# Two transformer-like layers: layer 0's output products in two pieces around the second head's turning, layer 1's first products in another order, layer 1's outputs through ScalarE

## The chip, the core and the metric

The kernel runs on one core of one Trainium2 chip. The metric is the device time of one launch in microseconds (us); the time before is the median of three runs. One more execution was recorded by the hardware profiler, and all times of single instructions come from it.

## What is computed

All values are float32, 4 sequences of 512 tokens (2048 in all) with 512 features. Two layers each add an attention and a mixture of experts to x:

```
xn = layernorm(x)
x  = x + attention0(xn) + experts0(xn)      # layer 0
xn = layernorm(x)
x  = x + attention1(xn) + experts1(xn)      # layer 1
```

- attention0 has 16 heads of 128. Queries, local keys and values are projections of xn with RMS norm and rotation. Each head adds two contexts: a softmax over the 8 best of the compressed entries (each entry stands for 4 tokens), and a softmax over the window of the last 128 tokens. The mean of both goes through the output matrix Wo: `out = merged @ Wo + bo`.
- experts0 takes the two best of 8 experts for each token, each one matrix, weighted by a softmax.
- attention1 is plain softmax attention with 16 heads of 32: `out = ctx @ wo_w.T + wo_b`.
- experts1 is again two of 8 experts with silu, a projection of the mix, the addition of x, and an RMS norm.

## The kernel before, in words

Tokens lie in 16 row tiles of 128. TensorE multiplies and also transposes by a product with the identity; results come out in PSUM, which has 8 banks of 128 x 512 float32. VectorE (V, DVE in the profile), ScalarE (A, ACT) and GpSimd (G, POOL) empty them. Every engine works through its own list of instructions in order. A scheduler makes these lists from the program's order and moves instructions among each other within an engine, apart from those pinned by `keep_in_program_order`. Additional work (norms, logits, experts, mixing) is put in by `run0((i, place))` in layer 0 and `run1((g, kc))` in layer 1, which run the jobs written down for that place.

**Layer 0** is the loop at L1020 over 32 steps: 8 groups of 2 heads (HG = 2), and for each the 4 sequences. Three kinds of PSUM tile are used: "mm" (3 banks), "sc" (3), "tr" (2) (L73). A step makes scores and contexts of its two heads and, between them, the projections of the next step by seven smaller products (`product`, L661, in "mm"; first to fifth). Its end is what the change touches, in this order:
- `turn_context(i, 0)`: four transposes of the first head's context (L820, trc, in "tr"), and one ScalarE copy into cT (L821).
- `fourth()` and `fifth()` of the next step, with the turnings of its queries and keys (L681, L687). In steps 5 to 23 `fifth()` stands behind these turnings, elsewhere in front. `fifth()` makes the products p3 in two halves (c = 0, 1), each added into lv by VectorE (L725), which frees its bank; then four squares with a sum on ScalarE (sq_k, L564), and the rotation on VectorE (L573 to L576). In steps 0 and 1, compressed keys and values of a sequence (kv, L609) are made nearby too.
- `turn_context(i, 1)` for the second head, `run0((i, 3.5))`.
- `output(i, t)` for the four row tiles t: two accumulating products, head 0 and head 1 (L828; each is two matmul instructions in the profile), into one "mm" bank, and VectorE's add into acc (L831).

A bank of a kind is taken again when the tile three before it (for "mm") has been emptied.

**The passage to layer 1** (L1429 on): PSUM is divided anew: "mm" 3 banks, "cx" 1, and 2 double ones, "st". `values(b, t)` is the value projection of a row tile (L1146, added out by L1148). `next_layer(n)` gives a pair of functions: the norm's rows on VectorE (L221 to L236), with wo_b added by GpSimd and the tile stored, and the turning of the normalised tile (trx, L242, copied out by ScalarE, L243). `second_logits(b)` issues the router's products (L252) and their copy (L254), and returns the function that turns them (trg, L259) and adds them up on VectorE (L867, L868). L1115 and L1116 are VectorE sums of weight matrices that must have landed first (wkT among them). 

**Layer 1's main loop** is over 16 groups of 4 heads and 4 blocks of keys: scores (st, L1224), the exponential on ScalarE (pT, L1226), context (cx, L1238), the sums of the weights on VectorE (L1244), queries and keys of a coming group (qp, L1200, emptied by L1204 to L1208). At the fourth block of groups 5 to 15, `output1(b, t)` makes one row tile of the attention's output: four products (o, L1307), then `add_part` (L1296), in which VectorE adds the PSUM tile to x, fetched by DMA before (`bring`, L1292). One more call follows the loop; that makes 12. The last four tiles are made otherwise (L1477, L1488). Jobs put in between mix the experts' rows: two gathers by DMA, L1340 and L1341 on VectorE, the turning (trc, L1349, copied out by L1353), the projection (po, L1360), the add L1361 that empties it, the square on ScalarE (L1364), two steps on GpSimd (L1365, L1366), L1371 on VectorE, and `add_part` again. All of o, po, qp, trc and sm share the three "mm" banks.

Of the kernel before, what the change touches and what calls it, by code (L numbers as in the profile page):

```python
# [12 lines left out]
F32 = mybir.dt.float32  # L13
I32 = mybir.dt.int32
AF = mybir.ActivationFunctionType
ALU = mybir.AluOpType
# [4 lines left out]
P = 128  # L21
B, S, HID = 4, 512, 512
T = B * S
NT = T // P
TC = S // P
# [11 lines left out]
HG = 2  # L37
# [12 lines left out]
def two_layers(ctx: ExitStack, tc: tile.TileContext, a: dict, out: bass.AP, large: bass.AP):  # L50
# [4 lines left out]
    V, G, A, PE = nc.vector, nc.gpsimd, nc.scalar, nc.tensor  # L55
# [17 lines left out]
    def psum(tag, name):  # L73
        return ps.tile([P, 512], F32, tag=tag, name=name, bufs={"mm": 3, "sc": 3, "tr": 2}[tag])
# [32 lines left out]
    def load_out(g):  # L107
        wo = wpool.tile([P, HG, HID], F32, tag="Wo", name=f"Wo_{g}", bufs=1)
        nc.sync.dma_start(out=wo, in_=a["Wo"][ds(g * HG * D, HG * D), :].rearrange("(h p) c -> p h c", p=P))
        return wo  # L110
# [12 lines left out]
    sums_w, out_w = {}, {}  # L123
# [3 lines left out]
    acc = keep.tile([P, NT, HID], F32, tag="acc", name="acc")  # L127
# [87 lines left out]
    def layernorm(n, pool, bank, scaled=False):  # L215

        pin = tc.keep_in_program_order if n < TC else (lambda x: x)
        st = small.tile([P, 6], F32, tag="st", name=f"st_{n}")  # L220
        pin(V.bn_stats(st, acc[:, n, :]))  # L221
        mv = small.tile([P, 2], F32, tag="mv", name=f"mv_{n}")
        V.bn_aggr(mv, st)
        V.tensor_scalar(mv[:, 1:2], mv[:, 1:2], 1e-5, None, ALU.add)
        G.tensor_tensor(mv[:, 1:2], mv[:, 1:2], nhalf[:, 0:1], ALU.pow)
        if scaled:
            G.tensor_scalar(mv[:, 0:1], mv[:, 0:1], mv[:, 1:2], -1.0, ALU.mult, ALU.mult)
        made = {}

        def rows():  # L230
            tag = "ctx" if n in (2, 3) else "xn"
            xn = made["xn"] = (wk0 if n in (2, 3) else pool).tile([P, HID], F32, tag=tag, name=f"xn_{n}")
            if scaled:
                A.activation(xn, acc[:, n, :], AF.Identity, scale=mv[:, 1:2], bias=mv[:, 0:1])
            else:
                pin(V.tensor_scalar(xn, acc[:, n, :], mv[:, 0:1], mv[:, 1:2], ALU.subtract, ALU.mult))  # L236
            (nc.scalar if TC <= n < 2 * TC else nc.sync).dma_start(out=xnd[ts(n, P), :], in_=xn)

        def turn():
            xn, tr = made["xn"], bank("tr", f"trx_{n}")  # L240
            for k in range(KC):
                pin(PE.transpose(tr[:, ts(k, P)], xn[:, ts(k, P)], ident))  # L242
            A.copy(xnT[:, :, ts(n, P)], tr.rearrange("p (k t) -> p k t", k=KC))  # L243
        return rows, turn


    def logits(b, w, m, pool, name, get, bank):


        lp = bank("sc", f"lg_{name}_{b}")  # L250
        for k in range(KC):
            PE.matmul(lp[ts(k, FEW), :], lhsT=w[:, k, :], rhs=xnT[:, k, ts(b, S)], start=True, stop=True)  # L252
        lr = pool.tile([P, S], F32, tag="lr", name=f"lr_{name}_{b}", bufs=1)
        A.copy(lr, lp)  # L254

        def turn():
            tr = bank("tr", f"trg_{name}_{b}")
            for t in range(TC):
                PE.transpose(tr[:, ts(t, P)], lr[:, ts(t, P)], ident)  # L259
            get(tr.rearrange("p (t k m) -> p t m k", k=KC, m=FEW)[:, :, 0:m, :])  # L260
        return lr, turn
# [555 lines left out]
    def turn_context(i, h, ctx_, cT):  # L817
        tr = psum("tr", f"trc_{i}_{h}")
        for t in range(TC):
            PE.transpose(tr[:, ts(t, P)], ctx_[:, t, :], ident)  # L820
        A.copy(cT[:, h, :], tr)  # L821

    def output(i, t, cT):
        g, b = steps[i]
        wo = out_w[g]
        op = psum("mm", f"op_{g}_{b}_{t}")
        for h in range(HG):
            PE.matmul(op, lhsT=cT[:, h, ts(t, P)], rhs=wo[:, h, :],  # L828
                      start=(h == 0), stop=(h == HG - 1))
        n = b * TC + t  # L830
        V.tensor_tensor(acc[:, n, :], acc[:, n, :], op, ALU.add)  # L831

    def combine(ex, n):
        rs = ex.gather(n)
# [29 lines left out]
    def second_logits(b, pool, bank):  # L864
        def get(rows_):
            own = lg1[:, ts(b, TC), :]
            V.tensor_reduce(own, rows_, AX.X, ALU.add)  # L867
            V.tensor_tensor(own, own, rout["rb"].unsqueeze(1).to_broadcast([P, TC, E]), ALU.add)  # L868
        return logits(b, rout["rw"], E, pool, "r1", get, bank)[1]
# [8 lines left out]
    for b in range(1, B):  # L878
        i = b - 2
# [58 lines left out]
    def next_layer(n, pool, bank):  # L938
        make_rows, turn_ = layernorm(n, pool, bank)

        def rows():
            make_rows()

            G.tensor_tensor(acc[:, n, :], acc[:, n, :], rout["wo_b"], ALU.add)
            nc.sync.dma_start(out=accd[ts(n, P), :], in_=acc[:, n, :])
        return rows, turn_
# [10 lines left out]
    for n in range(3 * TC):  # L957
        i, t = 29 + n // TC, n % TC
# [61 lines left out]
    for i, (g, b) in enumerate(steps):  # L1020
        if b == 0:
            if g:
                out_w[g] = load_out(g)
            if g + 1 < NH // HG:
                groups[g + 1] = load_later(g + 1)
        more = i + 1 < len(steps)
        turn_last = turn_keys
        now = qkT
        cT = qp.tile([P, HG, S], F32, tag="cT", name=f"cT_{g}_{b}", bufs=1)
        nc.sync.dma_start(out=cv0s[i % 2][96:P, 0:D], in_=cv[0:32, b, 0:D])  # L1030
        em0, lT0 = scores(i, 0, now)
        turn_last(1)
        if more:
            load_sums(i + 1)
            qkT, sums_x, first, second, third, fourth, fifth, turn_queries, turn_keys = project(i + 1)
            first()
            sums_x()
            if b == 2 and g + 1 in groups:
                groups[g + 1][0][0] = load_block(g + 1, "wA")
        run0((i, 0))  # L1040
        em1, lT1 = scores(i, 1, now)
        sT0 = turn(i, 0, em0)
        run0((i, 1))
        if more:
            second(0)
            turn_queries(0)
        ctx0 = context(i, 0, lT0, sT0, lv)
        if more:
            second(1)
        sT1 = turn(i, 1, em1)  # L1050
        if more:
            third()
        if b == 2 and g + 1 in groups:
            combine_weights(g + 1)
        run0((i, 2))
        ctx1 = context(i, 1, lT1, sT1, lv)
        turn_context(i, 0, ctx0, cT)
        run0((i, 3))
        if more:
            fourth()  # L1060

            for f in (lambda: turn_queries(1), lambda: turn_keys(0), fifth) if 5 <= i < 24 else (fifth, lambda: turn_queries(1), lambda: turn_keys(0)):
                f()
        turn_context(i, 1, ctx1, cT)
        run0((i, 3.5))
        for t in range(TC):
            output(i, t, cT)
        run0((i, 4))
    scratch.close()
    layer0.close()  # L1070
# [6 lines left out]
    ap_ = ctx.enter_context(tc.tile_pool(name="att1", bufs=2))  # L1077
    scratch = ctx.enter_context(ExitStack())
    rp = scratch.enter_context(tc.tile_pool(name="route1", bufs=1, side="right"))
# [18 lines left out]
    bank1 = lambda tag, name: psum1("mm", name)[:, 0, :]  # L1098
# [42 lines left out]
    def values(b, t):  # L1141
        if t == 0:
            v[b] = ap_.tile([P, TC, HID], F32, tag="v", name=f"v1_{b}")
        vp = bank1("mm", f"vp_{b}_{t}")
        for k in range(KC):
            PE.matmul(vp, lhsT=xnT[:, k, ds(b * S + t * P, P)], rhs=wa["wvT"][:, k, :],  # L1146
                      start=(k == 0), stop=(k == KC - 1))
        V.tensor_tensor(v[b][:, t, :], vp, rows["wv_b"], ALU.add)  # L1148
# [145 lines left out]
    def add_part(n, part_, way):  # L1294
        x = lies.pop((n, way))
        V.tensor_tensor(x, x, part_, ALU.add)  # L1296
        left[n] -= 1
        if left[n] == 0:
            nc.sync.dma_start(out=out_v[n], in_=x)
        elif (n, 1 - way) not in lies:  # L1300
            nc.sync.dma_start(out=accd[ts(n, P), :], in_=x)

    def output1(b, t):
        n = b * TC + t
        op = bank1("mm", f"o1_{n}")
        for jj in range(NJ):
            PE.matmul(op, lhsT=cT1[b][:, jj, ts(t, P)], rhs=wa["woT"][:, jj, :],  # L1307
                      start=(jj == 0), stop=(jj == NJ - 1))
        add_part(n, op, 0)

    r1 = Routing("r1", lg1, rp, const, bank1)
    held = {}
# [103 lines left out]
        jobs1.append((place, lambda t=t: values(1, t)))  # L1416
    run1 = schedule(jobs1)

    values(0, 0)
    norm = [next_layer(3 * TC + t, rp, bank1) for t in range(2)]  # L1420
    norm[0][0]()
    values(0, 1)
    turn_ = second_logits(B - 2, rp, bank1)
    norm[0][1]()
    norm[1][0]()
    norm.append(next_layer(3 * TC + 2, rp, bank1))
    values(0, 2)
    turn_()
    norm[1][1]()  # L1429
    norm[2][0]()  # L1430
    norm.append(next_layer(3 * TC + 3, rp, bank1))
# [7 lines left out]
    for g in range(NG):  # L1439
        b, j = groups1[g]  # L1440
# [743 lines left out]
```

## Time and profile before

| | us |
|---|---|
| three runs | 2075.61, 2073.08, 2073.09 |
| median | 2073.09 |
| the profiled execution | 2074.66 |
| its span, first to last instruction | 2072.6 |
| TensorE busy in it | 2017.7 (97%) |
| VectorE, ScalarE, GpSimd busy | 1452.0, 867.9, 754.3 |
| mean granted TensorE clock | 0.995 |

Lines of the profile begin with the line of the kernel (L828), then engine, operation and out<-in. In a timeline the first number is the start, the second the duration of the row (several instructions where it ends in x16), and the bracket tells how long the engine was idle before it and which instruction ended that. In the list of waits the three numbers are the total in us, how often, and the longest. A row of a window gives its bounds and length, then the busy us and number of instructions of PE, PEld (weight loads), DVE, ACT and POOL, the granted clock, the DMA share and GB/s.

### The profile page before, as it was taken

The page shows a single profiled execution, that of the slowest core. Times are in us where ns is not written, and L with a number is a line of the kernel's source. Part 1 is how long each engine was busy: PE and PEld are TensorE (multiplying, and loading weights), DVE is VectorE, ACT ScalarE, POOL GpSimd, SP SyncE. Part 2 cuts the span into 40 slices and gives each one's busy share as a digit, 9 for nine tenths or more (in the row PEclk, how much of TensorE's full clock was granted, in tenths as well). Part 3 has the DMA queues.
Part 4 walks back from the last instruction along what each step waited for, and adds up shares of the span by engine and source line. Part 5 has one row for each costly group of instructions (what it writes and reads, how often), then busy time and mean ns, then how long its engine had stood idle before and what let it go on. Part 6 is the DMA issues. An engine that isn't in the chain of part 4 may idle for free.

```text
span 2072.6 us, 27984 instructions
## 1 busy us (share of the span) xinstructions
PE 2017.7 (97%) x9130; PEld 1205.3 (58%) x9130; DVE 1452.0 (70%) x3543; ACT 867.9 (42%) x2600; POOL 754.3 (36%) x761
## 2 busy tenths in 40 slices
PE   6999999999999999999999999999999999999997
PEld 4666666666666666666666666666334445445442
DVE  7888967666766666676667778787596555557775
ACT  4554444444444443444444455454243432333332
POOL 4422244443423333344333444353114332332550
PEclk9999999999999999999999999999999999999999
DMA  7102133333333343234443222121317765773551
GB/s 250 68 31 62 42 118 120 143 108 103 130 130 104 109 155 103 92 135 166 183 170 116 70 76 85 42 72 62 119 51 244 263 243 196 257 243 123 158 163 52
DMA packets 98906, 267.23 MB, mean 129 GB/s; under 512 B 14400, under 2 KB 27840, under 8 KB 87488
## 3 DMA queue, kind: packets, MB, share of 16 engines
q0 software_dynamic: 27072, 148.91, 21.4%
q1 hardware_dynamic: 70528, 114.34, 16.4%
q10 hardware_dynamic: 1152, 2.10, 0.3%
q8 instruction: 75, 1.23, 0.2%
q14 instruction: 79, 0.65, 0.1%
HBM read 222.05 MB, written 42.73 MB: 128 GB/s over the span
## 4 chain that ended last, share of the span: by engine, by line
PE 81%; DVE 8%; ACT 3%; POOL 2%; DMA 2%; issue 1%; SPq 0%; ACTq 0%; POOLq 0%; DVEq 0%
PE p L661 23%; PE hp_r L518 12%; PE op L828 10%; PE st L753 4%; PE st L1224 3%; PE qp L1200 3%; PE sp L744 3%; PE cx L1238 2%; PE ca L797 2%; PE o L1307 2%; PE trm_r L506 2%; PE vp L1160 1%; PE trq L681 1%; PE trk L687 1%; PE cc L800 1%
## 5 line engine op out<-in xcount | busy, mean ns | idle before, releaser
L828 PE MATMUL op<-Wo,cT 128*128 128x512 f32 x512 | 230.6, 598 | 5.3 <-DVE lv L725 2.9
L518 PE MATMUL hp_r<-we_r,xT_r 128*128 128x512 f32 (+1 forms) x592 | 224.8, 596 | 0.0
L470 POOL DMA_INDIRECT xr_r<-xnd,rows_r x72 | 89.4, 1242 | 331.6 <-PE trm_r L506 298.2
L761 POOL TENSOR_TENSOR lT<-lT,lmask 128x512 f32<-128x512 f32 (+1 forms) x128 | 157.6, 1244 | 140.8 <-ACT lT L757 140.6
L661 PE MATMUL p<-wT,x 128*128 128x384 f32 x512 | 179.6, 493 | 0.5 <-DVE wT L119 0.5
L661 PE MATMUL p<-wB,x 128*128 128x384 f32 x512 | 175.9, 488 | 4.0 <-DVE u L717 4.0
L661 PE MATMUL p<-wA,xnT 128*128 128x384 f32 x512 | 174.0, 492 | 0.2 <-DVE u L696 0.2
L828 PEld LDWEIGHTS op<-Wo,cT 128*128 128x128 f32 x512 | 92.0, 190 | 115.0 <-issue 77.2
L564 ACT ACTIVATE sq<-qb 128x128 f32<-128x128 f32 x384 | 118.9, 310 | 93.0 <-DVE qb L710 44.9
L1226 ACT ACTIVATE pT<-st 128x1024 f32<-128x1024 f32 x128 | 123.7, 1014 | 62.7 <-PE st L1224 57.0
L518 PEld LDWEIGHTS hp_r<-we_r,xT_r 128*128 128x128 f32 (+1 forms) x592 | 83.8, 170 | 97.3 <-issue 91.8
L831 DVE TENSOR_TENSOR acc<-acc,op 128x512 f32<-128x512 f32 x128 | 87.4, 685 | 69.4 <-PE op L828 69.0
L661 PEld LDWEIGHTS p<-wB,x 128*128 128x128 f32 x512 | 93.9, 190 | 68.5 <-issue 10.2
L661 PEld LDWEIGHTS p<-wT,x 128*128 128x128 f32 x512 | 94.5, 193 | 63.5 <-issue 6.7
L661 PEld LDWEIGHTS p<-wA,xnT 128*128 128x128 f32 x512 | 95.6, 193 | 61.0 <-issue 2.9
L675 ACT ACTIVATE qb<-qb,ss 128x128 f32<-128x128 f32 x256 | 81.9, 390 | 110.7 <-POOL ss L566 108.6
L508 ACT COPY xT_r<-trm_r 128x512 f32<-128x512 f32 x72 | 41.8, 581 | 198.0 <-PE hp_r L518 188.3
L757 ACT ACTIVATE lT<-st,ss 128x256 f32<-128x256 f32 (+1 forms) x128 | 47.2, 449 | 175.4 <-PE st L753 175.3
L753 PE MATMUL st<-qkT 128*128 128x256 f32 (+1 forms) x512 | 110.4, 357 | 0.0
L534 POOL DMA_INDIRECT row_r<-yd,slot_r x64 | 74.2, 1160 | 94.0 <-DVE row_r L1341 35.8
L753 PEld LDWEIGHTS st<-qkT 128*128 128x128 f32 x512 | 93.1, 193 | 11.4 <-issue 1.4
L566 POOL TENSOR_TENSOR ss<-ss,nhalf 128x6 f32<-128x6 f32 x64 | 95.7, 1496 | 5.3
(360 smaller groups left out, 4334.2 us busy)
## 6 DMA issues: line engine op xcount, KB each, us to landing
x<-xsd SPq DMA_DIRECT2D x112, 256.0 KB, 3.1
yd<-yr_r SPq DMA_DIRECT2D x72, 256.0 KB, 3.4
wA<-in_wA SPq DMA_DIRECT2D x16, 384.0 KB, 3.6
wB<-in_wB SPq DMA_DIRECT2D x16, 384.0 KB, 7.6
xnd<-xn SPq DMA_DIRECT2D x24, 256.0 KB, 2.0
accd<-acc SPq DMA_DIRECT2D x18, 256.0 KB, 2.0
acc<-in_x SPq DMA_DIRECT2D x16, 256.0 KB, 4.9
Wo<-in_Wo SPq DMA_DIRECT2D x8, 512.0 KB, 3.6
```

The lines of the kernel that those rows point to most:

```text
L470: G.indirect_dma_start(out=out, out_offset=None, in_=src, in_offset=at_rows(idx))
L518: PE.matmul(hp[ts(h, m), :], lhsT=xT[:, k, ts(h, m)], rhs=w[:, ts(k, HID)], start=(k == 0), stop=(k == KC - 1))
L534: G.indirect_dma_start(out=x, out_offset=None, in_=self.yd, in_offset=at_rows(self.r.slot[:, k, n : n + 1]))
L564: A.activation(sq, x[:, h, :], AF.Square, accum_out=ss[:, h : h + 1])
L566: G.tensor_tensor(ss, ss, nhalf[:, 0:n], ALU.pow)
L661: PE.matmul(p, lhsT=x[:, k, ts(c, P)], rhs=w[:, k, :], start=(k == 0), stop=(k == 1))
L675: A.activation(x[:, j, :], x[:, j, :], AF.Copy, scale=sq[t][:, j : j + 1])
L753: PE.matmul(st[:, ds((t % 2) * 256, n)], lhsT=qkT[:, HG + h, ts(t, P)], rhs=qkT[:, h, ds(t * P, n)], start=True, stop=True)
L761: G.tensor_tensor(dst, dst, lmask.rearrange("p a w j -> p (a w j)")[:, 0:n], ALU.mult)
L828: PE.matmul(op, lhsT=cT[:, h, ts(t, P)], rhs=wo[:, h, :], start=(h == 0), stop=(h == HG - 1))
L831: V.tensor_tensor(acc[:, n, :], acc[:, n, :], op, ALU.add)
L1226: A.activation(pt[:, ts(pair, 2), :], st, AF.Exp, scale=SCALE1)
```

## The change

Three parts. In layer 0, `output` makes one head's product at a time and keeps the tile open between: the first-head products of row tiles 0 and 1 stand ahead of the second head's turning, that of tile 2 behind it, that of tile 3 between the second-head products of tiles 2 and 3. Three "mm" banks are open at once in that stretch. At the passage to layer 1, the first two norms are built ahead of the first value product, the logits of the third sequence are issued ahead of the second value product, and turned right behind it. In layer 1, ScalarE copies each of the 12 output tiles to SBUF, into a buffer of its own (one for all), and VectorE adds from there.

```
-    def output(i, t, cT):
+    open_ = {}
+
+    def output(i, t, h, cT):
+
         g, b = steps[i]
-        wo = out_w[g]
-        op = psum("mm", f"op_{g}_{b}_{t}")
-        for h in range(HG):
-            PE.matmul(op, lhsT=cT[:, h, ts(t, P)], rhs=wo[:, h, :],
-                      start=(h == 0), stop=(h == HG - 1))
-        n = b * TC + t
-        V.tensor_tensor(acc[:, n, :], acc[:, n, :], op, ALU.add)
+        if h == 0:
+            open_[t] = psum("mm", f"op_{g}_{b}_{t}")
+        PE.matmul(open_[t], lhsT=cT[:, h, ts(t, P)], rhs=out_w[g][:, h, :], start=(h == 0), stop=(h == HG - 1))
+        if h == HG - 1:
+            n = b * TC + t
+            V.tensor_tensor(acc[:, n, :], acc[:, n, :], open_.pop(t), ALU.add)
...
+
+        output(i, 0, 0, cT)
+        output(i, 1, 0, cT)
         turn_context(i, 1, ctx1, cT)
+        output(i, 2, 0, cT)
         run0((i, 3.5))
         for t in range(TC):
-            output(i, t, cT)
+            if t == 3:
+                output(i, t, 0, cT)
+            output(i, t, 1, cT)
         run0((i, 4))
...
-        add_part(n, op, 0)
+        o = ap_.tile([P, HID], F32, tag="o", name=f"o1s_{n}", bufs=1)
+        A.copy(o, op)
+        add_part(n, o, 0)
...
+    norm = [next_layer(3 * TC + t, rp, bank1) for t in range(2)]
     values(0, 0)
-    norm = [next_layer(3 * TC + t, rp, bank1) for t in range(2)]
     norm[0][0]()
+    turn_ = second_logits(B - 2, rp, bank1)
     values(0, 1)
-    turn_ = second_logits(B - 2, rp, bank1)
+    turn_()
     norm[0][1]()
     norm[1][0]()
     norm.append(next_layer(3 * TC + 2, rp, bank1))
     values(0, 2)
-    turn_()
     norm[1][1]()
```

## The prediction

> **What bounds the kernel.** I read the page first (busy shares, groups), then TensorE's waits, then timelines of single places. The first two lines of this fence are from the page, the rest from TensorE's waits (us in total, times, longest).
>
> ```profile
> PE 2017.7 (97%) x9130; PEld 1205.3 (58%) x9130; DVE 1452.0 (70%) x3543; ACT 867.9 (42%) x2600; POOL 754.3 (36%) x761
> ...
> L828 PE MATMUL op<-Wo,cT 128*128 128x512 f32 x512 | 230.6, 598 | 5.3 <-DVE lv L725 2.9 <-ACT cT L821 2.3
> ...
> PE op L828 <- DVE lv L725: 2.9, 4, 0.7
> PE op L828 <- ACT cT L821: 2.3, 5, 1.1
> PE po L1360 <- DVE acc L1296: 2.1, 1, 2.1
> PE qp L1200 <- DVE xnT L1296: 2.0, 1, 2.0
> PE vp L1146 <- ACT xnT L243: 1.4, 2, 0.7
> PE trc L820 <- ACT cT L821: 1.3, 1, 1.3
> ```
>
> TensorE is 97% busy, with 2072.6 - 2017.7 = 54.9 us idle, and the change adds or drops no TensorE instruction. In the two compiled orders SyncE's DMA issues stand as they stood, and GpSimd moves only a few normalisation steps. So the time moves only by the idle that it opens or closes, and by the granted clock. All waits that it could aim at are in that list: 5.3 in front of the outputs, 1.3 in front of the turnings, 4.1 behind layer 1's adds, and some 1.4 + 0.8 at layer 1's start: about 13 us, 0.6%. A matmul of 512 columns follows the one before by 0.43 us (16 of L828 take 6.9), one of 128 by 0.11. I use these paces.
>
> **Layer 0, steps 5 to 22 (18 steps): 0.** The timelines of step 10 (start, us, engine, what), first TensorE, then VectorE, then ScalarE:
>
> ```profile
> 544.69 0.81 PE L661 MATMUL p<-wB,x 128*128 128x384 f32 x2
> 545.34 0.60 PE L820 MATMUL trc<-ident,ctx 128*128 128x128 f32 x4
> 545.77 7.11 PE L828 MATMUL op<-Wo,cT 128*128 128x512 f32 x16
> ...
> 545.54 0.56 DVE L725 TENSOR_TENSOR lv<-p,u 128x384 f32<-128x384 f32 x1 [0.36 <-PE p L661]
> ...
> 545.97 0.59 ACT L821 COPY cT<-trc 128x512 f32<-128x512 f32 x1 [0.29 <-PE trc L820]
> 546.45 0.31 ACT L564 ACTIVATE sq_k<-lv 128x128 f32<-128x128 f32 x1
> ```
>
> Now, the second head's copy (L821, ends 546.56) is covered by tile 0's first-head product (0.86 from 545.77, to 546.63): hardly any stall. After, two products (1.72) run from 545.34 to 547.06, the turning to 547.50, tile 2's product to 548.36. The copy starts when ScalarE is through the four squares, which now stand ahead of it: one of them is held until 546.10 by L725, then three at 0.44 each end near 547.5. It starts at 547.8 (0.3 behind the turning), ends at 548.4: the same stall within 0.1. The three open tiles take all three "mm" banks. Tile 1 needs the bank of p3's first half (L725 ended at 545.18, wanted at 546.20), tile 2 the second's (546.10, wanted at 547.50): both in time. The last add falls where it fell. Bounds: ±0.1 a step, 18 steps, **±1.8**; I take 0, as every wanted time above has slack but the copy's.
>
> **Steps 0 and 1: +2.5.** Here the compressed keys and values (kv, L609) lay around the turning; the change puts outputs ahead of them. TensorE, then VectorE, in step 0:
>
> ```profile
> 91.72 0.60 PE L687 MATMUL trk<-ident,qb 128*128 128x128 f32 x4
> 92.16 0.39 PE L609 MATMUL kv<-wk,entT 128*128 128x128 f32 x2
> 92.56 0.66 PE L820 MATMUL trc<-ident,ctx 128*128 128x128 f32 x4
> 93.05 0.83 PE L609 MATMUL kv<-wk,entT 128*128 128x128 f32 x6
> 93.72 1.06 PE L609 MATMUL kv<-wv,entT 128*128 128x128 f32 x8
> 94.62 7.24 PE L828 MATMUL op<-Wo,cT 128*128 128x512 f32 x16
> ...
> 94.01 1.01 DVE L725 TENSOR_TENSOR lv<-p,u 128x384 f32<-128x384 f32 x2
> ```
>
> VectorE reaches L725 only at 94.01, behind L718, L719 and L652. After, tile 0 starts at 92.16 and ends its first product at 93.02, tile 1 waits for L725's first half, about 94.57: 1.5 of idle, queued in front of the turning and of kv, which used to fill it. From there 14 output matmuls (6.0) and 4 + 16 of the short ones (2.2) end near 102.8 instead of 101.7: **+1.1**. In step 1 (turning of keys ended at 138.59, L725 at 140.74) the same working ends at 149.3 instead of 147.9: **+1.4**; two transposes ahead of tile 1 fill 0.2 of it. Bounds: 0, if the stall is taken from a later wait, to +1.6 each. I take the near-full price, as VectorE waits on TensorE at the end of both steps (1.03 in front of the last add of each) and so has nothing to give back.
>
> **Other steps: +0.8.** Step 2: +0.16. Step 4: -0.36 (its turning waits 0.7 on L682 now; a product covers that). Step 23: -0.29. In 24, 25, 27 and 28 to 31 the product between was there already, and the longer way through tile 2 puts the second-head copy behind more squares or norms: +0.12 x 3, +0.48, +0.35, +0.08, +0.05. Sum **+0.8**, bounds -0.7 (only the gains) to +1.5 (only the losses). Layer 0: **+3.3**.
>
> **Layer 1's start: +0.3.** Both norms are built and the logits issued before the second values product. The turning at 1462.94 waits 0.83 for the copy of the logits (L254) and the values at 1464.27 wait 0.68 for L243; the values product (3.6) that moves ahead covers the first. But the logits' second turning (L259) then stands early, and its bank is emptied on VectorE by L867, now queued behind L1115. L1115 runs at 1461.54 and 1462.80 because wkT lands at 1461.5. So the norm's turning gets its bank near 1464.4 and the next values start at 1465.7. Against that, the wait of 0.80 at 1469.21 for xn goes. The third values product starts where it did within 0.1; with the last outputs of step 31 later, **+0.3**; bounds -1.6 (both covered waits gone) to +2.0 (all waits replaced by VectorE's queue).
>
> **Layer 1's outputs through ScalarE: -1.2.** Twelve copies of 128x512 at 0.58 (the row of L821 and L1353) are 7 us on an engine 42% busy, beside TensorE; the next ScalarE operation behind outputs 0 to 6 comes 4.1 later, so nothing queues behind the copy there. For these the add, too, already comes 0.2 after the matmuls: 0. If the cover went (ScalarE late by a whole copy), it would be 12 x 0.58 = 7 at most. Output 8 is where it can pay:
>
> ```profile
> 1972.40 0.68 DVE L1296 TENSOR_TENSOR xnT<-xnT,o 128x512 f32<-128x512 f32 x1
> 1973.00 0.67 DVE L1361 TENSOR_TENSOR xa<-xa,po 128x512 f32<-128x512 f32 x1
> 1973.13 3.12 PE L1200 MATMUL qp<-xnT,wqT 128*128 128x256 f32 x8 [2.01 <-DVE xnT L1296]
> ...
> 1974.00:1977.50 3.50, 3.50 (x10) 2.77 (x9) 0.74 (x1) 3.07 (x6) 2.42 (x4) 0.54 0.86 260
> ```
>
> The tile was ready at 1964.5, but VectorE stood in L1361, L1371 and L1244 until 1972.40, and qp waited 2.01 for the bank. The last line is one window: the granted clock is 0.54 behind that wait, which costs about 1.7 us more. After, the copy is due behind the two Exps that end at 1967.47, long before qp wants the bank (1971.1). But the next two qp tiles need the bank of the projection emptied by L1361, which stays behind the add, at 1973.7, and the gather's row sums end at 1980. I count 1.2 of the 3.7 as kept. Output 9 is alike: po waits 2.13 at 2016.60; after, it starts at 2014.4, but the following projection needs L1361 at 2023.41 to 2024.09 as now (it starts at 2024.23 today): all is lost again. Bounds: -5.8 (2.0 + 1.7 + 2.1 all kept) to +2 (nothing kept, and one low-clock stretch of 1.7 in the now longer idle at 2024). I take **-1.2**, nearer to the row of L1361.
>
> On the clock, the trace first: a wait of 2.01 was followed by 3.4 us at about half clock, one of 2.13 was not. [...]
>
> **Sum.** +3.3 + 0.3 - 1.2 = **+2.4** against the profiled execution, 2074.66 (span 2072.6 and 2.06 around it): 2077.1. That one lies 1.57 over the median of the three runs, so the median moves from 2073.09 to **2075.5**. 0.2%, about what a measurement can tell from no change, is 4.1 us: 2068.9 to 2077.2.
>
> **Rivals.**
> - Covers replace each other, as summed: 2075.5, chance 0.50, own range 2071.5 to 2077.2. This holds also the case that hardly anything moves (2073).
> - **Banks and squares decide (slower)**, 0.33. With three tiles open, any lateness of L725 or of the four squares stops TensorE in each of 18 steps, with the turning queued behind it. For it: copy and demand meet within 0.1 in my working. Against: L725 has 1.0 to spare. At 0.2 a step it is 3.6 more, 2079.1; it decides from 0.1 a step (1.8, with the 2.4: 2077.3). A low-clock stretch behind the 1.5 us stalls of steps 0 and 1, 1.7 each, comes to the same.
> - **Layer 1 keeps its gain (faster)**, 0.17: -5.8, with steps 0 and 1 absorbed later and the -0.7 of the other steps: 2073.1 - 6.5 = 2066.6. For it: each freed bank is one that TensorE waited for by name. Against: L1361 and the gathers stand where they stood.
>
> The range 2069.5 to 2080.5 takes in the first case and the nearer half of both others.
>
> **What would show it.** Right: L828 waits for L725 about 1.5 in each of steps 0 and 1, and kv runs behind it; in steps 5 to 22 the stall ahead of the second head stays under 0.1; the 2.0 at qp and 2.1 at po go, and new waits on L1361 follow within 10 us. Wrong: a wait on L821 near 0.3 in each step (slower), or a layer 1 shorter by over 3 us (faster).

## The result and the profile after

The changed kernel takes 2077.95 us (median of 16 runs, 2075.9 to 2080.85) against 2073.66 for the kernel before (16 runs, 2071.7 to 2076.01): a ratio of 1.0020, 95% interval 1.0012 to 1.0027. It is slower by 4.3 us, just over the 0.2% that was set as the bound. The forecast was 2.4 us.

First the costliest group of the page of the changed kernel, then its TensorE waits (total, times, longest) that answer to those shown of before:

```profile
L830 PE MATMUL op<-Wo,cT 128*128 128x512 f32 x512 | 236.0, 599 | 10.0 <-DVE lv L725 7.9
```

```profile
PE op L830 <- DVE lv L725: 7.9, 8, 1.5
PE po L1370 <- DVE xa L1371: 2.5, 3, 1.5
PE op L830 <- ACT cT L821: 2.1, 3, 1.3
PE trc L1359 <- DVE qk L1213: 1.4, 1, 1.4
...
PE vp L1154 <- ACT xnT L243: 1.3, 2, 0.7
...
PE trc L1359 <- DVE qk L1221: 1.1, 2, 0.9
```

The change aimed at three kinds of wait. The waits of qp and po behind layer 1's adds (2.0 and 2.1) are gone, and waits on L1371, L1213 and L1221 have come: 5.0 us at po and trc, and 0.7 more at qp, where before only L1361 had 1.6 at po:

```profile
PE po L1360 <- DVE xa L1361: 1.6, 3, 0.6
```

The wait of the turning on L821 (1.3) is gone from that name and now stands at an output product. And the outputs wait 7.9 for L725, where it was 2.9.

To see where it went, I cut TensorE's time at five points that every kernel has. The first stretch runs from the first matmul to the end of step 1's outputs, the passage from step 31's last output to the first scores of layer 1 (L1224 of before), the loop from there to the last matmul. A run of matmuls is taken to end 0.43 after its last start (16 of L828 take 6.9 in the kernel before), and the last matmul counts by its start. All numbers are us, from the profiled execution of each kernel; those below "changed" are the experiments.

| kernel | to end of step 1 | steps 2 to 27 | 28 to 31 | passage | loop | ratio of times (95%) |
|---|---|---|---|---|---|---|
| before | 142.03 | 1154.93 | 148.41 | 31.44 | 582.32 | |
| changed | 146.39 | 1154.10 | 150.13 | 32.33 | 581.14 | 1.0020 (1.0012 to 1.0027) |
| layer 0 part only | 145.22 | 1154.18 | 150.41 | 32.68 | 581.35 | 1.0016 (1.0007 to 1.0025) |
| passage only | 141.60 | 1154.95 | 148.64 | 30.24 | 580.40 | 0.9996 (0.9986 to 1.0005) |
| copies only | 141.85 | 1154.92 | 149.49 | 31.45 | 581.85 | 0.9999 (0.9990 to 1.0007) |
| changed, steps 0 and 1 as before | 142.23 | 1154.40 | 150.13 | 33.09 | 582.55 | 1.0002 (0.9993 to 1.0011) |
| changed, other banks in steps 0 and 1 | 141.63 | 1154.12 | 150.14 | 33.02 | 581.42 | 1.0005 (0.9996 to 1.0014) |
| copies only, adds on GpSimd | 141.40 | 1154.92 | 152.90 | 31.45 | 585.13 | 1.0024 (1.0014 to 1.0034) |
| pieces in 4 to 23, and passage | 141.77 | 1154.15 | 149.39 | 30.26 | 581.07 | 0.9991 (0.9982 to 1.0000) |
| the same, turning ahead of p3 | 143.66 | 1153.62 | 148.15 | 30.25 | 580.67 | 0.9982 (0.9973 to 0.9991) |

A column can be read against itself: kernels whose code agrees in a stretch show how far it varies by chance. Steps 2 to 27 repeat within 0.03 in the kernels that have the old code there, the passage within 0.02 where no low clock falls into it. With the code of before, the first stretch varies by some 0.8 in all but the last row, steps 28 to 31 by 1.1 (by 4.5 with the run with adds on GpSimd), and the loop without copies by 1.9. In the last row's first stretch, whose code is that of before, TensorE waits 1.6 for L596 at 71 us, where the kernel before has no wait.

Now the places. In the changed kernel's timeline of step 0, first TensorE, then VectorE:

```profile
93.64 1.02 PE L830 MATMUL op<-Wo,cT 128*128 128x512 f32 x2
96.11 1.12 PE L830 MATMUL op<-Wo,cT 128*128 128x512 f32 x2 [1.44 <-DVE lv L725]
97.07 0.60 PE L820 MATMUL trc<-ident,ctx 128*128 128x128 f32 x4
97.51 1.02 PE L830 MATMUL op<-Wo,cT 128*128 128x512 f32 x2
98.37 1.05 PE L609 MATMUL kv<-wk,entT 128*128 128x128 f32 x8
...
95.50 1.01 DVE L725 TENSOR_TENSOR lv<-p,u 128x384 f32<-128x384 f32 x2
```

Tile 0's product runs, tile 1's waits 1.44 for the bank that L725 empties, and the turning and all of kv are queued behind it. Set instruction against instruction, TensorE's lag behind the kernel before grows by 1.23 in step 0 and 1.53 in step 1. (It had already lost 1.5 before step 0, in the head of the kernel, where nothing was changed.) From step 5 to step 22 the lag stays at 3.81 throughout.

The steady step 10 of the changed kernel, TensorE and then the one copy on ScalarE:

```profile
549.14 1.88 PE L830 MATMUL op<-Wo,cT 128*128 128x512 f32 x4
550.86 0.60 PE L820 MATMUL trc<-ident,ctx 128*128 128x128 f32 x4
551.29 5.40 PE L830 MATMUL op<-Wo,cT 128*128 128x512 f32 x12
...
551.50 0.58 ACT L821 COPY cT<-trc 128x512 f32<-128x512 f32 x1 [0.23 <-PE trc L820]
```

Tile 2's first-head product (551.29 to 552.15) covers the copy (551.50 to 552.08), and the second head's run follows. From the first output or turning of the stretch to the scores it was 7.38 before (545.34 to 552.72); it is 7.39 now (549.14 to 556.53).

The passage, first two rows of the kernel before, then the changed kernel's TensorE, its VectorE ahead of the first wait, and the window behind the two waits:

```profile
1452.66 0.66 PE L242 MATMUL trx<-ident,xn 128*128 128x128 f32 x4 [0.80 <-DVE xn L236]
1469.21 0.66 PE L242 MATMUL trx<-ident,xn 128*128 128x128 f32 x4 [0.80 <-DVE xn L236]
...
1458.22 0.66 PE L242 MATMUL trx<-ident,xn 128*128 128x128 f32 x4 [1.19 <-DVE xn L236]
1459.55 5.40 PE L1154 MATMUL vp<-wvT,xnT 128*128 128x512 f32 x8 [0.67 <-ACT xnT L243]
...
1470.46 0.66 PE L242 MATMUL trx<-ident,xn 128*128 128x128 f32 x4 [0.45 <-DVE lg L869]
...
1456.43 0.69 DVE L221 BATCH_NORM_STATS2 st<-acc 128x6 f32<-128x512 f32 x1
1457.03 0.67 DVE L833 TENSOR_TENSOR acc<-acc,op 128x512 f32<-128x512 f32 x1
1457.62 0.54 DVE L236 TENSOR_SCALAR xn<-acc,mv 128x512 f32<-128x512 f32 x1
...
1460.00:1463.50 3.50, 3.50 (x6) 1.36 (x5) 0.00 (x0) 0.00 (x0) 0.52 (x2) 0.53 1.03 355
```

The first wait was 0.80 before (at 1452.66). The eight matmuls behind it take 5.4 instead of 3.6, and the granted clock is 0.53 there: nothing of the kind stood in the passage of before, where it is 1.00 from 1447 to 1463.

### The profile page after: what moved, and what is told of

Its sections match the earlier page's. It is cut to its first block, busy times and chain, and to the rows that moved or that the text cites. A ratio compares the mean times of both kernels' runs of the same rounds, so it can differ in the third digit from the quotient of the medians.

```text
span 2077.3 us, 27995 instructions
## 1 busy us (share of the span) xinstructions
PE 2019.2 (97%) x9130; PEld 1203.3 (58%) x9130; DVE 1452.5 (70%) x3543; ACT 876.3 (42%) x2612; POOL 755.5 (36%) x761
## 3 DMA queue, kind: packets, MB, share of 16 engines
q8 instruction: 75, 1.23, 0.2%
## 4 chain that ended last, share of the span: by engine, by line
PE 77%; DVE 8%; ACT 3%; POOL 2%; DMA 2%; issue 1%; SPq 0%; DVEq 0%; ACTq 0%; POOLq 0%
PE p L661 21%; PE hp_r L518 12%; PE op L830 10%; PE st L753 4%; PE st L1232 3%; PE qp L1208 3%; PE sp L744 2%; PE cx L1246 2%; PE ca L797 2%; PE o L1315 2%; PE trm_r L506 2%; PE vp L1168 1%; PE vp L1154 1%; PE trq L681 1%; DVE pS L1252 1%
## 5 line engine op out<-in xcount | busy, mean ns | idle before, releaser
L830 PE MATMUL op<-Wo,cT 128*128 128x512 f32 x512 | 236.0, 599 | 10.0 <-DVE lv L725 7.9
```

Source lines behind the costliest of these rows:

```text
L830: PE.matmul(open_[t], lhsT=cT[:, h, ts(t, P)], rhs=out_w[g][:, h, :], start=(h == 0), stop=(h == HG - 1))
```

## Layer 0's part alone, and the passage alone

**Layer 0's part** is the first two hunks of the change, on the kernel before.

> Only layer 0's part of the change. In the changed kernel's trace TensorE falls behind the kernel before by 1.2 us in step 0 and 1.5 in step 1, gains 0.4 each in steps 4 and 23, loses nothing in steps 5 to 22, and loses about 1.7 in steps 28 to 31. Theory (products ahead of the compressed keys' matmuls wait for a bank that VectorE frees late): all of that comes here, +3.2 to +3.6 us. Rival 1 (a new stall in each of 18 steps): the loss grows evenly over steps 5 to 22, over +4. Rival 2 (the loss is the chip's start, which has nothing to do with the change): about 0 beside the start.

Ratio 1.0016 (1.0007 to 1.0025). The lag grows by 1.27 in step 0 and 1.54 in step 1, shrinks by 0.44 over steps 2 to 4 (0.32 of it in step 4) and by 0.38 in step 23, stays flat in steps 5 to 22, and grows by 2.0 in steps 28 to 31. That is the theory's list, and no stall in each step. One thing was not on it: the passage, whose code is that of before here, takes 32.68 instead of 31.44, with the wait of 1.19 for L236 (0.80 before) and a low clock behind it (0.55 in the 3.4 us from 1458.60).

**The passage** is the last hunk alone.

> Only the passage to layer 1. Theory (the covered wait for the logits' copy returns as a wait for VectorE's L867): between +0.3 and +0.9, too little to see in the median, to be read from the trace as TensorE's lag behind the kernel before at the first queries of layer 1. Rival (this part is a gain that the late norms of layer 0's last step spoiled in the full change): -0.8 or better at that place.

The passage takes 30.24 instead of 31.44: **the rival was right**, this part gains 1.2 by itself. Its TensorE rows:

```profile
1452.44 0.65 PE L242 MATMUL trx<-ident,xn 128*128 128x128 f32 x4 [0.80 <-DVE xn L236]
1453.77 3.70 PE L1146 MATMUL vp<-wvT,xnT 128*128 128x512 f32 x8 [0.68 <-ACT xnT L243]
...
1462.98 0.66 PE L242 MATMUL trx<-ident,xn 128*128 128x128 f32 x4 [0.45 <-DVE lg L867]
```

The wait for L867 that I had expected is there, but at 0.45, since the scheduler puts L867 behind only the first of the two L1115 in this kernel; and the wait for xn at the next turning (0.80 before, at 1469.21) is gone. In the three kernels that hold all three parts, L867 (then L869) stands behind both, as I had read it from the changed kernel's order. In the two later kernels with this part and without the copies it stands behind the first only, so the copies go with the other order; no run has this part and the copies alone. The two experiments below that hold all three parts show what that costs: VectorE's rows in the first of them (the sums have line 1130 there),

```profile
1462.97 1.23 DVE L1130 TENSOR_TENSOR acc<-wkT 128x1024 f32<-128x1024 f32 x1 [0.98 <-DMA wkT<-in_wkT]
1464.23 1.23 DVE L1130 TENSOR_TENSOR acc<-acc,wqT 128x1024 f32<-128x1024 f32 x1
1465.37 0.28 DVE L869 TENSOR_REDUCE lg<-trg_r 128x32 f32<-128x128 f32 x1
```

and a wait of 1.23 for L869 at the turning, against 0.45 here. The changed kernel's own 0.45 only says that TensorE came late to the turning, in the low clock. So the parts don't add up: the gain of 1.2 belongs to this part alone, with another order on VectorE.

## The copies alone

Only the hunk in `output1`.

> Only the 12 copies through ScalarE. Theory (the wait of 2.0 at qp and of 2.1 at po go, and most comes back as waits on L1361 and on the row sums of the gathers): -1.0, between -0.5 and -1.5, at the end, with a lead of about 2.5 for some 8 us behind output 8. Rival 1 (all freed): -3.7 to -5.8. Rival 2 (the copies delay the exponentials): +0.5 or more.

Ratio 0.9999 (0.9990 to 1.0007); the loop takes 581.85. The waits of 2.0 and 2.1 are gone here too, and TensorE's waits in the loop's last part (1900 to 2060 us) are these:

```profile
PE po L1362 <- DVE xa L1363: 2.4, 2, 2.0
PE trc L1351 <- DVE qk L1205: 2.2, 1, 2.2
PE sm L1252 <- DVE pS L1244: 0.7, 1, 0.7
PE qp L1200 <- DVE xa L1363: 0.7, 1, 0.7
```

The lead behind output 8 is there too (2.4 us in the stretch from 1970), and given back 10 us later. Over all kernels but the next one, the loop takes 582.32, 581.35, 580.40, 581.07 and 580.67 without copies (mean 581.2) and 581.14, 581.85, 582.55 and 581.42 with them (mean 581.7). So the copies change the names of the waits and no gain is left; -1.0 is not borne out. The spread of 1.9 among kernels without copies is larger than what was to be measured. Part of it is the clock: the five loops without copies had six stretches of 3.4 us at half clock, the four with copies two. With 1.7 us taken off for each (an estimate: half of 3.4), the loops take 577.3 to 580.6 without copies and 580.2 to 581.4 with them. So the copies seem to cost about what they save in low clock; no run separates the two.

To learn what holds these places, the adds behind the copies went to GpSimd. (It adds from the copy in SBUF. Other than the description of the kernel before has it, none of the 761 GpSimd instructions in its trace reads a PSUM tile: VectorE and ScalarE alone empty them.)

```
-    def add_part(n, part_, way):
+    def add_part(n, part_, way, V=V):
...
-        add_part(n, op, 0)
+        o = ap_.tile([P, HID], F32, tag="o", name=f"o1s_{n}", bufs=1)
+        A.copy(o, op)
+        add_part(n, o, 0, G)
```

> The 12 copies alone, and the adds behind them on GpSimd in place of VectorE. In all runs with copies so far the waits of 2.0 (qp) and 2.1 (po) went, and waits for L1361, L1205 and L1213 on VectorE of the same sum came. Theory A (VectorE's queue is the limit at outputs 8 and 9): without 0.68 of add ahead of L1361 the new waits shrink by 0.5 to 0.7 each, main loop 580 to 581. Theory B (the gathers and the chain of the norm set these places): the same waits within 0.3, or longer ones, as GpSimd's add (about 1.28) delays the gathers that it issues; main loop 582 or more.

Ratio 1.0024, loop 585.13: theory B. The waits of this kernel in the same part of the loop:

```profile
PE po L1362 <- DVE xa L1363: 3.5, 3, 2.5
PE trc L1351 <- DVE qk L1205: 2.7, 1, 2.7
PE trc L1351 <- DVE qk L1213: 2.3, 2, 1.2
```

Taking 0.68 of add from VectorE at each output did not shorten them. GpSimd's add at output 8 runs from 1979.32 to 1980.59, and the next gather that GpSimd issues begins only at 1980.75. So 0.68 less on VectorE is not enough to shorten these waits when 1.27 more stands in front of the gathers on GpSimd. The run changes both at once, so it doesn't show that VectorE's load has no part, and whether the gathers and GpSimd's chain also set these places in the kernel before was not tried. (Steps 28 to 31, whose code is that of before, also took 3.9 longer in this run than in the other four kernels with that code on average, with a low clock, 0.50 to 0.52 from 1438.20 to 1445.00, behind a wait of 1.89 for L770 in step 31.)

## Steps 0 and 1

The whole change, with the order of before for the first two steps:

```
+        if i >= 2:
             output(i, 0, 0, cT)
             output(i, 1, 0, cT)
             turn_context(i, 1, ctx1, cT)
...
+        else:
+            turn_context(i, 1, ctx1, cT)
+            run0((i, 3.5))
+            for t in range(TC):
+                output(i, t, 0, cT)
+                output(i, t, 1, cT)
+            run0((i, 4))
```

> The whole change, but steps 0 and 1 keep the order of before. Theory: 2.7 us less than the whole change, so about +0.6 against before beside the noise of the start; no wait of L830 on L725 in steps 0 and 1. Rival (the late time in steps 0 and 1 would have been lost at a later wait anyway): within 1 us of the whole change.

2074.54, ratio 1.0002 (0.9993 to 1.0011), against 1.0020 for the whole change; the first stretch is 142.23. The time lost in these two steps is not lost anyway: without it the kernel ends sooner.

Is it the bank, or the later place of kv? The same order, with other banks:

```
-            open_[t] = psum("mm", f"op_{g}_{b}_{t}")
+            open_[t] = psum("sc" if i < 2 and t in (1, 2) else "mm", f"op_{g}_{b}_{t}")
```

> The whole change, but in steps 0 and 1 the output tiles of row tiles 1 and 2 are put in two of the three banks for scores, which are empty there; the order of the instructions is meant to stay that of the change. Theory (the early products wait for the bank that VectorE's L725 empties): the waits of L830 on L725 in steps 0 and 1 (1.44 in step 0 of the changed kernel) go, and the two steps together take 141.9 to 142.5 us from the first matmul to the end of step 1 as in the kernel before, instead of 2.75 more. Rival (the loss comes from the compressed keys' matmuls standing later): the two steps stay as long as in the change.

The first stretch takes 141.63, and step 0 of this kernel reads:

```profile
92.41 1.88 PE L830 MATMUL op<-Wo,cT 128*128 128x512 f32 x4
94.13 0.60 PE L820 MATMUL trc<-ident,ctx 128*128 128x128 f32 x4
94.57 1.02 PE L830 MATMUL op<-Wo,cT 128*128 128x512 f32 x2
95.43 1.05 PE L609 MATMUL kv<-wk,entT 128*128 128x128 f32 x8
```

No wait is left, kv still stands behind three products, and L725 is as late as before (it starts at 94.27, in the kernel before at 94.01). So **the bank is the cause**, and the order alone costs nothing.

## Versions from the parts that gained

First the pieces only in steps 4 to 23, with the passage, without the copies.

> The products in two pieces only in steps 4 to 23, with the passage to layer 1 changed, without the copies. Theory (only the places that gained are kept): steps 2 to 27 take 1154.1 as in the change against 1154.93 before, steps 28 to 31 148.4 to 149.5 against 150.1 to 150.4, the passage about 30.2 as in the run with it alone, so -2.0 us and a ratio of 0.999. Rival (the passage's gain was chance): -0.8.

2072.25, ratio 0.9991 (0.9982 to 1.0000), as forecast, though the interval also holds the rival's 0.9996. The trace decides: the passage gains its 1.2 again. Steps 28 to 31 are back at 149.39, the wait at the passage's head at 0.80, and the passage at 30.26 with a granted clock of 1.00. So the longer wait at the head of the changed kernel's passage comes from the pieces in layer 0's last steps, and without the copies L869 again costs 0.45.

Most of the remaining waits of the outputs stand in steps 23, 24, 25 and 27, on L725 and on the copy behind the squares. So both were taken out of the way: the early products, the turning and its copy ahead of `fifth`, row tiles 1 and 2 in banks for scores.

```
+            if 23 <= i < 31:
+                output(i, 0, 0, cT)
+                output(i, 1, 0, cT)
+                turn_context(i, 1, ctx1, cT)
+                output(i, 2, 0, cT)
             for f in (lambda: turn_queries(1), lambda: turn_keys(0), fifth) if 5 <= i < 24 else (fifth, lambda: turn_queries(1), lambda: turn_keys(0)):
...
-            open_[t] = psum("mm", f"op_{g}_{b}_{t}")
+            open_[t] = psum("sc" if 23 <= i < 31 and t in (1, 2) else "mm", f"op_{g}_{b}_{t}")
```

> The run with steps 4 to 23 and the passage changed, and in steps 23 to 30 the early products, the turning and its copy now stand ahead of fifth (the products p3), with row tiles 1 and 2 in banks for scores; so neither a bank held by L725 nor ScalarE's four squares stand in front of the second head. Theory (these two are what the outputs of steps 23 to 25 and 27 to 29 wait for): the waits of 0.7 on L725 and 0.3 on L821 per step of the kernel before go, about 1.0 in each of steps 23, 24, 25 and 27 and 0.3 in 28 and 29; steps 2 to 27 take 1150.5 to 1151.5 us, and the time is about 4 us less than that run's, near 2068.5, ratio 0.997. Rival (p3's results are then late for the next step, which waits for its keys instead): at most 1 us less than that run, with new waits of TensorE on L682, L688 or L725 in these steps.

2071.11, ratio 0.9982 (0.9973 to 0.9991): faster than both kernels. But it gained less than the theory said. Steps 2 to 27 take 1153.62, 0.5 less than the run before it, and not 3; steps 28 to 31 take 148.15. (The passage's first wait is 0.80 here too, with pieces up to step 30, so the 1.19 comes with those of step 31.) Its waits in steps 2 to 27 (147 to 1300 us):

```profile
PE op L830 <- ACT cT L821: 4.7, 6, 1.0
...
PE op L830 <- DVE lv L725: 0.7, 1, 0.7
```

L725's wait is down from 3.5 in the run before to 0.7; in its place the products wait for the copy of the *first* head, about 0.8 in each of steps 23, 24, 25 and 27, and 0.99 in step 26, where no output had waited: moved forward, they came too early for it. Neither theory had this wait.

## Why the prediction was right, and where it was not

The time lies in the range, on the forecast side, at 4.3 us where 2.4 were summed. It also lies above the main case's own range (2077.95; that range ended at 2077.2), where the rival of banks and squares would have put it. So the time alone doesn't speak for the main case: the steps do.

- **Steps 5 to 22, 0: right.** The lag is constant at 3.81 over all of them. The rival of a stall in each step is out.
- **Steps 0 and 1, +2.5: right**, at 1.23 + 1.53 = 2.76. L725's bank is shown by the run with other banks, and "VectorE has nothing to give back" by the run without these steps.
- **Other steps, +0.8: near in sum (+0.4), wrong in three places.** Steps 2 to 27 gained 0.83. Of this 0.32 came in step 4 and 0.39 in step 23, as forecast, and 0.15 in step 2, where I had +0.16. Steps 24, 25 and 27, for which I had counted +0.36, cost 0. A longer wait for L725 (1.14 against 0.71 in step 24) took the place of the wait of 0.31 for the copy, not the sum of both. Steps 28 to 31 cost more than the 0.96 I had: 150.2 on the mean of four kernels, against 149.0 on the mean of the four kernels before, passage only, copies only and pieces in 4 to 23, so 1.2. Step 31 makes this mean uncertain: with its old code, one wait there (for L770) is 0.36, 0.35, 1.45 and 1.32 in these four. Up to step 30 the cost is clearer: the lag grows by 1.3 to 1.5 over steps 28 to 30 in the four kernels with the pieces, by 0 to 0.24 in the others. What makes it up was not tried.
- **Passage, +0.3: the step that failed.** It loses 0.9 in the changed kernel, and 1.6 in the two other kernels with all three parts. One wait is the one that I had: L869 is queued behind both sums. The other I did not have: in layer 0's last step the adds come close together, two rows of L221 stand ahead of the last one (1457.03), and L236 follows late (1.19 instead of 0.80). Less the clock's 1.7, those two kernels would be at about 31.4, as before. What I left out is the clock: it fell to half for some 3.4 us in all four kernels with layer 0's part in steps 28 to 31 (0.50 from 1460.23 to 1463.64 in the changed kernel). I had named such a stretch as a possible price of the 1.5 us stalls in steps 0 and 1, where none came (the clock is 1.00 from 67.59 to 1460.23).
- **Copies, -1.2: right in kind, wrong in size.** Both waits went, and waits for the projection's bank and behind the rows took their place, as described; but nothing was left. I had counted part of the gain from the low clock behind qp's wait in the one profile of before. It isn't a fixed part of that kernel: the run with layer 0's part alone has the same wait of 2.0 at qp and no low clock there (1.00 from 1961.80 to 1982.20). That the two loops in the table differ by just the forecast's 1.2 (582.32 and 581.14) is luck: the one low-clock stretch of before, 3.41 us at 0.50 and so about 1.7, is more than all of it.

The sum by the traces, an estimate: 2.8 - 0.8 + 1.2 + 1.4 (mean of the three kernels with all parts) + 0.5 = 5.1, within the interval of the measured 4.3 (2.5 to 5.6).

## What to carry to other kernels

When a product is moved ahead, look up who empties the bank that it will take and how late that engine runs at this place; what is queued behind the product waits with it, and another pool's free bank can undo the whole loss (here the first stretch took 146.39 us in the changed kernel and 141.63 with other banks). Moving work of equal length past a copy cost nothing where the copy is covered on both sides (7.38 us before, 7.39 after, in step 10), so look at the first and last iterations, whose neighbours differ. A single profile's low-clock stretch is not a fixed cost of the wait in front of it: in the kernel before it came behind a wait of 2.01 us and not behind one of 2.13. Look also at waits that lie close together: 1.19 and 0.67 within 2.5 us had a low clock behind them in two executions of four.

## What the runs showed of the hardware

In the passage the low clock came behind waits that lie close together, and not in every execution. It was profiled ten times:

- Waits of 0.80 (0.81 in one) and 0.68 within 2.3 us (before, and five experiments): in none of the six a low clock behind them.
- Waits of 1.19 and 0.67 (the changed kernel and three experiments with layer 0's part): followed by some 3.4 us at half clock in the changed kernel and with layer 0's part alone, not in the other two. Those two had a second pair, of 1.23 and 0.67 in one and of 1.14 and 0.67 in the other, and the low clock behind that one. With 0.45 in place of 1.23 (three kernels) there was none.
- In the loop, single waits of about 2.0 were followed by a low clock in some executions and not in others: behind the 2.01 at qp the clock was 0.50 in the kernel before (1973.84 to 1977.25), and 1.00 behind the same wait in the run with layer 0's part alone.

This is the second pair in the run with steps 0 and 1 as before, TensorE:

```profile
1465.71 0.66 PE L242 MATMUL trx<-ident,xn 128*128 128x128 f32 x4 [1.23 <-DVE lg L869]
1467.04 5.38 PE L1161 MATMUL vp<-wvT,xnT 128*128 128x512 f32 x8 [0.67 <-ACT xnT L243]
```

The eight matmuls take 5.38, the next eight (from 1472.70) 3.60; by rows of 0.5 us the clock was 1.00 until 1467.0, 0.50 from 1467.5 to 1470.0 and 1.00 from 1470.5. So in the ten passages 1.8 to 1.9 us of idle within 2.6 us had a low clock behind it in four of six cases, and 1.5 had none.

Where the low clock begins can be read from the traces of the kernel before and of the changed one. It falls to 0.50 at 24.83, 62.38, 1973.84 and 2069.41 in the first, and at 23.22, 64.18, 1460.23 and 2074.63 in the second. Counted from the first of them, these are 11, 571 and 599, and 12, 421 and 601 times 3.41333 us, within 0.01. I cut both traces into pieces of that length, laid by these starts: from 80 us to the last matmul there are 580 and 582. The clock was low right behind two of them, which held 2.01 (before, from 1970.43) and 1.87 us (changed, from 1456.82) of TensorE idle. Of the other 1160 only one held more than 1.53: 1.80, in the kernel before from 2014.80. These pieces, each with the next one; first the two of before, then the one of the changed kernel:

```profile
1970.43:1973.84 3.41, 1.40 (x11) 0.66 (x4) 3.25 (x5) 0.07 (x1) 2.18 (x2) 1.00 0.65 198
1973.84:1977.25 3.41, 3.41 (x9) 2.68 (x9) 0.49 (x1) 3.23 (x6) 2.58 (x4) 0.50 0.86 256
...
2014.80:2018.21 3.41, 1.61 (x4) 0.87 (x5) 2.25 (x3) 1.07 (x3) 1.73 (x2) 1.00 0.67 234
2018.21:2021.63 3.42, 3.42 (x17) 1.38 (x15) 1.44 (x2) 2.55 (x4) 1.32 (x3) 1.00 0.86 282
...
1456.82:1460.23 3.41, 1.54 (x8) 0.86 (x7) 2.31 (x8) 1.17 (x2) 2.47 (x4) 1.00 0.61 177
1460.23:1463.64 3.41, 3.41 (x6) 1.36 (x5) 0.14 (x1) 0.00 (x0) 0.29 (x1) 0.50 1.04 364
```

The wait of 2.13 at po began at 2014.47, so that a part of it lies ahead of the piece from 2014.80, and the clock stayed at 1.00. In the first 80 us less idle stood in front of a low clock: 1.50 from 58.96 in the kernel before (0.50 from 62.38) and 1.43 from 60.76 in the changed one (0.50 from 64.18). So the idle in one piece does not tell by itself whether the clock falls, and what else enters was not shown.
